# A recurrent kernel's step: two gates in one PSUM bank, wider products, and another order on VectorE

## The chip, the cores and the metric

The kernel runs on one core of a Trainium2 chip. TensorE (PE) multiplies, with its weight loads in a queue of their own (PEld); VectorE (DVE) and ScalarE (ACT) do the elementwise work; GpSimd (POOL) and SyncE (SP) start transfers. PE writes its sums to PSUM, which has eight banks of 512 float32 values in each of 128 partitions. The metric is the device time in microseconds of one execution, as the median of several runs. Everything is in float32.

## The reference

`x` is 16 sequences of 256 steps with 512 features. A GRU runs over the steps from a given state, and a router with 16 experts (one shared weight matrix) works on all of its states. Cut to what matters:

```python
def cell(h, x):
    gi = x @ W_ih + b_ih
    gh = h @ W_hh + b_hh
    i_r, i_z, i_n = jnp.split(gi, 3, axis=-1)
    h_r, h_z, h_n = jnp.split(gh, 3, axis=-1)
    r = sigmoid(i_r + h_r)
    z = sigmoid(i_z + h_z)
    n = tanh(i_n + r * h_n)
    return (1.0 - z) * n + z * h

# then, on the states as 4096 rows of 512:
S = softmax(states @ router_w + router_b)       # 16 experts
G, idx = top_k(S.T, 256)                        # each expert takes 256 rows
y[idx] += G * (states[idx] @ expert_w + expert_b)
return x + y
```

The 256 steps depend on each other: the products `h @ W_hh` of a step need the state that the step before it made.

## The kernel before, in words

**The state's form.** The 512 features are four chunks of 128, and `hs` holds the state with the features on the partitions: `hs[:, k, slot, :]` is chunk k for the 16 sequences. It is the stationary operand, with 16 columns, and `W_hh` is streamed past it. A product with 16 or 32 columns fills only a strip of PE's array, so `h_part` issues four products with `tile_position=(0, 32*j)`, one per strip of 32 columns. Strip j makes every fourth block of 32 output features (`columns`), and its result lies in partitions 32j onward. The 512 features of one gate thus lie as 128 partitions by 128 columns.

Two steps share a set of sums: an even step uses 16 rows of each strip; the odd step after it gives PE both states (32 columns) and uses the other 16. `p, odd = divmod(s, 2)`; the sums of pair p are in column half `p % 2` of a bank. Before the change each gate has a bank: `r_bank`, `n_bank`, `z_bank`, of which columns 0 to 255 are used. `rr`, `hn`, `zz` are the two halves of each.

**What is added to the sums.** The part of x for a pair is made six pairs ahead by `x_part`, in products of 384 columns (three gates) into `x_bank0` or `x_bank1`, and `x_done` on DVE adds biases and puts it into a ring in SBUF. ACT copies it into the sums before the recurrent products add to them: `preset_first` for r, `preset_rest` for n's bias and for z. For n, x's part stays in the ring, since r multiplies only the recurrent part.

**One step.** The order on PE, ACT, DVE, POOL and SP in the step loop is the order of the calls (a manual schedule); the framework adds a semaphore wait wherever one engine needs another's result, or a place that another engine still uses. PE runs the first half of the contraction (chunks 0, 1, `first`) for r and for n, then the second half (`second`) for r and for n, and then all of z:

```python
for ks in (first, second):
    h_part(s, "r", ks)
    h_part(s, "n", ks)
h_part(s, "z", range(KC))
```

So the first products need only the first half of the state's features. After them PE does work that does not hang on this step: half of an `x_part` (L403) and, in most steps, one unit of an expert's product for an earlier group of states (`expert`, L370); some steps have router products instead (`logits`, L305).

ACT: sigmoid of r (L505), in even steps `preset_first` (L386), two tanh, one for each half of the features (L557), sigmoid of z (L558), in even steps `preset_rest` (L389, L396), in some steps a `gather` (L293).

DVE: `seen` (L509), a copy of a single value of r, so that DVE has waited for ACT before its next instruction waits for PE; r times n's sums by halves (L553); plus x's part (L555); and then ten small instructions, five for each half: `turn_n` transposes n in 32 by 32 blocks (L565), `turn_z` transposes z (L568), `less_n` makes h - n (L571), `by_z` multiplies by z (L576), `plus_n` adds n and writes the half of the next state (L579). After that come `x_done` in odd steps, an expert's results, and transposes of x.

POOL and SP: SP starts the loads of x, some of which POOL lets go by a small copy that reads the newest state (L219, L617).

**After the steps** the last router products, softmax, a search for each expert's 256th value, and the output follow; several expert products are left for then (`late_part`, L108).

Of the kernel before, what the change touches and what calls it, by code (L numbers as in the profile page):

```python
# [8 lines left out]
F32 = mybir.dt.float32  # L9
# [3 lines left out]
AF = mybir.ActivationFunctionType  # L13
# [4 lines left out]
def kernel(  # L18
# [15 lines left out]
    nc = tc.nc  # L34
    B, T, D = x.shape
    E = router_w.shape[1]
    P = 128
    QD = 32
    KC = D // P
# [118 lines left out]
    with (  # L158
# [9 lines left out]
        def slot(s):  # L168
# [3 lines left out]
        whh = wts.tile([P, KC, 3, D], F32, name="whh")  # L172
# [9 lines left out]
        ones = wts.tile([2, QD], F32, name="ones")  # L182
        nc.vector.memset(ones, 1.0)

        r_bank, n_bank, z_bank, x_bank0, x_bank1, l_bank = banks = [
            ps_g.tile([P, D], F32, name=f"gates{i}") for i in range(6)
        ]
        rr, hn, zz = ([bank[:, P * i : P * (i + 1)] for i in range(2)] for bank in (r_bank, n_bank, z_bank))
        lgt = l_bank[:, 0:P]

        def quadrant(j, m=QD):
            return slice(QD * j, QD * j + m)

        def columns(ap, j):

            return ap.rearrange("p (c j i) -> p j c i", j=KC, i=QD)[:, j]

        def load_rows(dst, src, form):

            rows = src.rearrange(form, c=KC)  # L200
            for h in range(2):
                ks = slice(KC // 2 * h, KC // 2 * (h + 1))
                queues[h].dma_start(out=dst[:, ks, :], in_=rows[:, ks, :])
# [33 lines left out]
        with tc.manual_schedule(engines={ET.SP, ET.Activation, ET.Pool}):  # L237
            def load_gate(dst, src, form, i, gate):
                load_rows(dst[:, :, i, :], src[:, gate * D : (gate + 1) * D], form)

            def load_k(k):
                rows = w_ih.rearrange("(p c) n -> p c n", c=KC)
                to = wih.rearrange("p c g d -> p c (g d)")
                for h, queue in enumerate(queues):
                    cols = slice(3 * HD * h, 3 * HD * (h + 1))
                    queue.dma_start(out=to[:, k, cols], in_=rows[:, k, cols])

            nc.sync.dma_start(out=xs[:, 0, :], in_=x[:, 0:TG, :])
            load_k(0)
            nc.scalar.dma_start(out=c0, in_=cond)  # L250
            load_k(1)
            load_k(2)
            nc.scalar.dma_start(out=xs[:, 1, :], in_=x[:, TG : 2 * TG, :])
            load_k(3)
            for gate in (0, 2, 1):
                load_gate(whh, w_hh, "(c p) n -> p c n", gate, gate)
            nc.scalar.activation(dummy, ones[0:1, 0:1], AF.Sigmoid)
            for dst, src in (
                (b_raw[0:1], b_ih.rearrange("(o g d) -> o g d", o=1, d=D)),
                (b_raw[1:2], b_hh.rearrange("(o g d) -> o g d", o=1, d=D)),  # L260
                (b_n, b_hh[2 * D :].rearrange("(o d) -> o d", o=1)),
            ):
                nc.gpsimd.dma_start(out=dst, in_=src)
            for j in range(KC):
                load_xa(2, xa2, j, (nc.sync, nc.sync))
            nc.sync.dma_start(out=ewr[:, :, E:], in_=expert_w.rearrange("(c p) n -> p c n", c=KC))
            nc.sync.dma_start(out=ewr[:, :, 0:E], in_=router_w.rearrange("(c p) n -> p c n", c=KC))
            nc.gpsimd.dma_start(out=rb, in_=router_b.rearrange("(o e) -> o e", o=1).to_broadcast([P, E]))
            nc.sync.dma_start(out=eb, in_=expert_b.rearrange("(o d) -> o d", o=1).to_broadcast([P, D]))
# [145 lines left out]
                ring[:, p % AHEAD, :, :], bank[:, 0 : 3 * P].rearrange("p (g d) -> p g d", d=P), bias[:, 0:3, :], ALU.add  # L415
            )

        def h_part(s, gate, ks):
            p, odd = divmod(s, 2)
            m = QD if odd else B  # L420
            dst, gate_ = {"r": (rr[p % 2], 0), "z": (zz[p % 2], 1), "n": (hn[p % 2], 2)}[gate]
            for k in ks:

                lhs = hs[:, k, slot(s) - odd : slot(s) + 1, :].rearrange("p t b -> p (t b)")
                for j in range(KC):
                    nc.tensor.matmul(  # L426
                        dst[quadrant(j, m)],
                        lhs,
                        columns(whh[:, k, gate_, :], j),
                        start=False,  # L430
                        stop=(k == KC - 1),
                        tile_position=(0, QD * j),
                        skip_group_check=True,
                    )
# [8 lines left out]
        with tc.manual_schedule(engines={ET.PE, ET.Activation, ET.DVE}):  # L443
            for bank in banks:
                begin_sums(bank)
            keep_clock(8)
            held = (r_bank, n_bank, z_bank, x_bank0, x_bank1)

            def spread_x(g, bank):
                xT[g] = xtp.tile([P, TG // 2, P], F32, name="xt")  # L450
                for c in range(KC):
                    nc.tensor.transpose(bank[:, P * c : P * (c + 1)], xs[:, g, c::KC], ident)
                for q in range(TG // 2):
                    to = xT[g][:, q, :].rearrange("p (c o b) -> p c o b", c=KC, b=B)
                    nc.vector.tensor_copy(
                        to, bank.rearrange("p (c b t) -> p c t b", c=KC, t=TG)[:, :, 2 * q : 2 * q + 2, :]
                    )

            spread_x(0, idles[0])
            keep_clock(2, (idles[1],))  # L460
            for k in range(KC):
                for p in range(KC):
                    x_part(p, k, held[p], start=False)
                if k == 1:
                    for c in range(KC):
                        nc.tensor.transpose(
                            idles[1][:, B * c : B * (c + 1)], c0[:, P * c : P * (c + 1)], ident[0:B, 0:B]
                        )
                    nc.vector.tensor_copy(
                        hs[:, :, 0, :], idles[1][:, 0 : KC * B].rearrange("p (k b) -> p k b", b=B)  # L470
                    )
                elif k == 2:
                    biases(l_bank)
                    nc.vector.tensor_copy(bias, l_bank.rearrange("p (g d) -> p g d", d=P))
            spread_x(1, idles[0])
            for p in range(KC):
                x_done(p, held[p])
                if p == 0:
                    preset_first(0)
                elif p == 2:  # L480
                    preset_rest(0)
            for k in range(KC):
                x_part(KC, k, held[KC], start=False)
            x_done(KC, held[KC])
            keep_clock(2)
# [3 lines left out]
        first, second = range(KC // 2), range(KC // 2, KC)  # L489

        with tc.manual_schedule(engines={ET.PE, ET.Activation, ET.DVE, ET.Pool, ET.SP}):
# [4 lines left out]
            for s in range(T):  # L496
                p, odd = divmod(s, 2)
                g, c = divmod(s, TG)
                for ks in (first, second):
                    h_part(s, "r", ks)  # L500
                    h_part(s, "n", ks)
                h_part(s, "z", range(KC))

                r = gp.tile([P, P], F32, name=f"r{odd}")
                nc.scalar.activation(r, rr[p % 2], AF.Sigmoid)  # L505
# [30 lines left out]
                if s >= T - 2:  # L536
                    expert_for(4)

                halves = [
                    (half, slice(QD * ks[0], QD * (ks[-1] + 1)), slice(ks[0], ks[-1] + 1))  # L540
                    for half, ks in enumerate((first, second))
                ]
                t, nT, zT = (
                    [gp.tile([P, P // 2], F32, name=f"{name}{half}") for half in range(2)]
                    for name in (f"t{odd}", "nT", "zT")
                )
# [1 line left out]
                    [gp.tile([P, KC // 2, B], F32, name=f"{name}{half}") for half in range(2)]  # L548
                    for name in ("u", "v")
                )  # L550
                zs = gp.tile([P, P], F32, name=f"zs{odd}")
                for half, cols, ks in halves:
                    nc.vector.tensor_tensor(t[half], r[:, cols], hn[p % 2][:, cols], ALU.mult)  # L553
                for half, cols, ks in halves:
                    nc.vector.tensor_tensor(t[half], t[half], ring[:, p % AHEAD, 2, cols], ALU.add)  # L555
                for half, cols, ks in halves:
                    nc.scalar.activation(t[half], t[half], AF.Tanh)  # L557
                nc.scalar.activation(zs, zz[p % 2], AF.Sigmoid)  # L558
                if not odd and p < T // 2 - 1:
                    preset_rest(p + 1)  # L560
                if g and c < KC:
# [3 lines left out]
                    nc.vector.transpose(nT[half], t[half])  # L565

                def turn_z(half):
                    nc.vector.transpose(zT[half], zs[:, halves[half][1]])  # L568

                def less_n(half):  # L570
                    nc.vector.tensor_tensor(  # L571
# [9 lines left out]
                    )  # L581

                for f, half in (
                    (turn_n, 0), (turn_n, 1), (less_n, 0), (turn_z, 0), (less_n, 1),
                    (by_z, 0), (plus_n, 0), (turn_z, 1), (by_z, 1), (plus_n, 1),
                ):
                    f(half)

# [24 lines left out]
                if cx >= KC and gx + 2 < NG:  # L613
                    if cx == KC:
                        xa_next = new_xa()
                    j = cx - KC
# [27 lines left out]
    with (  # L644
# [80 lines left out]
        with tc.manual_schedule(engines={ET.PE, ET.Activation, ET.DVE}):  # L725

            bank = ps_s.tile([P, D], F32, name="bank", tag="s")
# [42 lines left out]
            gate = gate_of(pg)  # L770
# [3 lines left out]
            for i, (g, cols) in enumerate(items):  # L774
# [4 lines left out]
                if step == 1:  # L779
                    n = ps_n.tile([P, 1], F32, name="n", tag="n")  # L780
# [14 lines left out]
        with tc.If(again > 0):  # L795
# [51 lines left out]
            gate = gate_of(pg)  # L847
# [39 lines left out]
```

## Time and profile before

| | |
|---|---|
| time, median of 3 runs | 1165.82 us (1165.52 to 1165.89) |
| the profiled execution: its own time, and the span of its trace | 1166.15 us, 1164.4 us |
| granted clock of TensorE | full in all slices of the span |
| from the first to the last sigmoid of r (255 steps apart) | 27.8 to 1089.9 us of the span |
| recurrent products, L426 | 24,576 of 128 columns, 724.7 us busy |
| x's part, L403 | 4,064 of 384 columns, 379.6 us busy |
| sigmoid of r, L505, and of z, L558 | 256 of each, 278 ns each |
| tanh, L557 | 512, 249 ns each |
| transposes of n, L565, and of z, L568 | 512 of each, 234 and 240 ns each |
| last sum, L579 | 512, 192 ns each |

The profile is of one execution. "Busy" counts time in which at least one instruction of the group was under way; neighbours overlap, so it is less than the number times the mean. Products on PE are pipelined, and a product that waits for its turn in the array is not told from one that runs. Therefore the distance between starts says more than busy time, and I use the recorded start of single instructions where a turn of the step loop is measured.

### The profile page before, as it was taken

What the parts mean: (1) busy time and instruction counts of PE and PEld (TensorE: products, weight loads), DVE (VectorE), ACT (ScalarE), POOL (GpSimd) and SP (SyncE); (2) the same over time, 40 slices, a digit from 0 to 9 for tenths busy, and PEclk for the clock granted to TensorE, in tenths of its full rate; (3) what the DMA queues carried; (4) which work ended last, traced back from release to release, by engine and by line L of the source; (5) the groups of instructions that cost most, each with busy time, mean ns of one, the idle gap of its engine ahead of it and who ended that gap; (6) DMA issues with size and microseconds to landing.
All of it is one profiled execution on the core that took longest, in us unless ns stands there. A gap on an engine that the chain in (4) does not pass through costs nothing.

```text
span 1164.4 us, 72051 instructions
## 1 busy us (share of the span) xinstructions
PE 1148.1 (99%) x32271; PEld 925.2 (79%) x32271; DVE 769.0 (66%) x4229; ACT 387.0 (33%) x1590; POOL 42.5 (4%) x240
## 2 busy tenths in 40 slices
PE   8999999999999999999999999999999999998898
PEld 4778888888888888888888888888888888888762
DVE  2666667666666666666676666666666666665674
ACT  1233333333333333333333333333333333333420
POOL 1000000000000000000000000000000000000000
PEclk9999999999999999999999999999999999999999
DMA  8100000000000000000000000000000000000126
GB/s 268 38 13 17 21 20 19 16 21 22 20 20 21 19 20 17 21 22 20 20 19 20 19 18 20 22 21 20 20 20 19 20 8 13 4 5 4 48 69 227
DMA packets 43818, 37.02 MB, mean 32 GB/s; under 512 B 6992, under 2 KB 35424, under 8 KB 43504
## 3 DMA queue, kind: packets, MB, share of 16 engines
q1 hardware_dynamic: 41808, 28.89, 8.4%
q8 instruction: 255, 4.18, 1.5%
q10 hardware_dynamic: 1568, 3.44, 0.9%
q14 instruction: 59, 0.48, 0.1%
q0 software_dynamic: 128, 0.02, 0.1%
HBM read 23.94 MB, written 8.39 MB: 28 GB/s over the span
## 4 chain that ended last, share of the span: by engine, by line
PE 95%; DVE 3%; DMA 1%; ACT 1%; issue 0%; SPq 0%; ACTq 0%; DVEq 0%
PE gates L426 57%; PE gates L403 27%; PE pe L108 5%; PE pe L370 5%; DMA wih<-in_L_cond_W_ih_dram 1%; PE gates L305 1%; DVE zT L568 0%; DVE nT L565 0%; DVE t L553 0%; ACT r L505 0%; ACT t L557 0%; DVE hs L579 0%; DVE v L576 0%; PE idle L403 0%; DVE u L571 0%
## 5 line engine op out<-in xcount | busy, mean ns | idle before, releaser
L426 PE MATMUL gates<-whh,hs 128*16 128x128 f32 x24576 | 724.7, 273 | 5.0 <-DVE zT L568 2.5
L426 PEld LDWEIGHTS gates<-whh,hs 128*16 128x16 f32 x24576 | 672.0, 103 | 37.6 <-ACT ht L293 15.8
L403 PE MATMUL gates<-wih,xt 128*32 128x384 f32 x4064 | 379.6, 486 | 1.9 <-DMA wih<-in_L_cond_W_ih_dram 1.6
L505 ACT ACTIVATE r<-gates 128x128 f32<-128x128 f32 x256 | 71.1, 278 | 551.9 <-PE gates L426 551.7
L403 PEld LDWEIGHTS gates<-wih,xt 128*32 128x32 f32 x4064 | 144.4, 110 | 91.4 <-issue 84.3
L509 DVE COPY seen<-r 1x1 f32<-1x1 f32 x256 | 36.3, 142 | 268.0 <-ACT r L505 267.9
L557 ACT ACTIVATE t<-t 128x64 f32<-128x64 f32 x512 | 103.2, 249 | 136.1 <-DVE t L555 136.1
L565 DVE STREAM_TRANSPOSE nT<-t 128x64 f32<-128x64 f32 x512 | 100.4, 234 | 47.8 <-ACT t L557 47.8
L568 DVE STREAM_TRANSPOSE zT<-zs 128x64 f32<-128x64 f32 x512 | 122.7, 240 | 0.6 <-ACT zs L558 0.6
L370 PEld LDWEIGHTS pe<-ewr,ht 128*32 128x32 f32 x1920 | 69.1, 110 | 62.3 <-issue 60.1
L579 DVE TENSOR_TENSOR hs<-v,nT 128x32 f32<-128x32 f32 x512 | 98.3, 192 | 17.4
L576 DVE TENSOR_TENSOR v<-u,zT 128x32 f32<-128x32 f32 x512 | 98.7, 193 | 8.8
L370 PE MATMUL pe<-ewr,ht 128*32 128x128 f32 x1920 | 92.0, 273 | 0.7 <-issue 0.7
L555 DVE TENSOR_TENSOR t<-t,xs 128x64 f32<-128x64 f32 x512 | 90.7, 219 | 0.0
L553 DVE TENSOR_TENSOR t<-r,gates 128x64 f32<-128x64 f32 x512 | 90.3, 218 | 0.0
L571 DVE TENSOR_TENSOR u<-hs,nT 128x32 f32<-128x32 f32 x512 | 78.2, 153 | 0.0
L558 ACT ACTIVATE zs<-gates 128x128 f32<-128x128 f32 x256 | 71.2, 278 | 1.8 <-ACT t L557 0.6
L414 DVE TENSOR_TENSOR xs<-gates,bias 128x384 f32<-128x384 f32 x127 | 69.7, 551 | 0.5 <-PE gates L403 0.5
L108 PE MATMUL pe<-ewr,ht 128*32 128x128 f32 (+2 forms) x1320 | 64.3, 343 | 0.0
L108 PEld LDWEIGHTS pe<-ewr,ht 128*32 128x32 f32 x1320 | 36.9, 110 | 20.5 <-issue 18.5
L293 ACT COPY ht<-hs 128x128 f32<-128x128 f32 (+1 forms) x128 | 52.2, 410 | 0.8 <-DVE hs L579 0.8
L228 DVE STREAM_TRANSPOSE xt<-xa 128x256 f32<-128x256 f32 x58 | 38.7, 668 | 6.5 <-issue 6.5
(106 smaller groups left out, 300.0 us busy)
## 6 DMA issues: line engine op xcount, KB each, us to landing
out_dram<-xs SPq DMA_DIRECT2D x31, 256.0 KB, 3.7
xa<-in_x_dram SPq DMA_DIRECT2D x232, 32.0 KB, 1.9
xs<-in_x_dram SPq DMA_DIRECT2D x100, 64.0 KB, 2.2
xs<-in_x_dram SPq DMA_DIRECT2D x6, 256.0 KB, 3.9
wih<-in_L_cond_W_ih_dram ACTq DMA_DIRECT2D x4, 384.0 KB, 7.9
wih<-in_L_cond_W_ih_dram SPq DMA_DIRECT2D x4, 384.0 KB, 10.7
whh<-in_L_cond_W_hh_dram SPq DMA_DIRECT2D x3, 512.0 KB, 12.8
whh<-in_L_cond_W_hh_dram ACTq DMA_DIRECT2D x3, 512.0 KB, 9.6
```

The source lines that it names most:

```text
L108: nc.tensor.matmul(pe[q, cols], ht[:, g, k, q], ewr[:, k, E:][:, cols], start=False, stop=(k == KC - 1), tile_position=(0, QD * j), skip_g ...
L370: nc.tensor.matmul(pes[g][quadrant(j), at : at + P], ht[:, g, k, quadrant(j)], ewr[:, k, E + P * quarter : E + P * (quarter + 1)], start=F ...
L403: nc.tensor.matmul(bank[quadrant(j), at], lhs, columns(wih[:, k, gates, :].rearrange("p g d -> p (g d)"), j), start=start and k == 0, stop ...
L426: nc.tensor.matmul(dst[quadrant(j, m)], lhs, columns(whh[:, k, gate_, :], j), start=False, stop=(k == KC - 1), tile_position=(0, QD * j), ...
L553: nc.vector.tensor_tensor(t[half], r[:, cols], hn[p % 2][:, cols], ALU.mult)
L555: nc.vector.tensor_tensor(t[half], t[half], ring[:, p % AHEAD, 2, cols], ALU.add)
L557: nc.scalar.activation(t[half], t[half], AF.Tanh)
L565: nc.vector.transpose(nT[half], t[half])
L568: nc.vector.transpose(zT[half], zs[:, halves[half][1]])
L571: nc.vector.tensor_tensor(u[half], hs[:, halves[half][2], slot(s), :], of_step(nT[half], odd), ALU.subtract)
L576: nc.vector.tensor_tensor(v[half], u[half], of_step(zT[half], odd), ALU.mult)
L579: nc.vector.tensor_tensor(hs[:, halves[half][2], slot(s + 1), :], v[half], of_step(nT[half], odd), ALU.add)
```

## The change

Three things are changed in the step, and one follows from them.

1. r and n of a pair share a bank. There are still two banks for them, but they are now told apart by the pair and not by the gate: `rn_bank0` holds r (columns 0 to 127) and n (128 to 255) of even pairs, `rn_bank1` those of odd pairs. `W_hh` is stored in the order r, n, z, so that r's and n's columns for a contraction chunk stand side by side. In the first contraction half `h_part(s, "rn", first)` then makes both in products of 256 columns. The second half is made apart as before, r ahead of n.
2. The last contraction chunk of z is made in two halves of 64 columns, first for the first half of the features. z's sigmoid is made in two instructions of 64 columns, and each stands behind the tanh of its half on ACT.
3. The ten small instructions on DVE have another order: the transpose of z's first half goes ahead of that of n's second half, and the other work on the second half later.

```diff
-        r_bank, n_bank, z_bank, x_bank0, x_bank1, l_bank = banks = [
+        rn_bank0, rn_bank1, z_bank, x_bank0, x_bank1, l_bank = banks = [
             ps_g.tile([P, D], F32, name=f"gates{i}") for i in range(6)
         ]
-        rr, hn, zz = ([bank[:, P * i : P * (i + 1)] for i in range(2)] for bank in (r_bank, n_bank, z_bank))
+        rn = [bank[:, 0 : 2 * P] for bank in (rn_bank0, rn_bank1)]
+        rr, hn = ([both[:, P * i : P * (i + 1)] for both in rn] for i in range(2))
+        zz = [z_bank[:, P * i : P * (i + 1)] for i in range(2)]
...
-            for gate in (0, 2, 1):
-                load_gate(whh, w_hh, "(c p) n -> p c n", gate, gate)
+            for i, gate in enumerate((0, 2, 1)):
+                load_gate(whh, w_hh, "(c p) n -> p c n", i, gate)
...
-        def h_part(s, gate, ks):
+        def h_part(s, gate, ks, half=None):
             p, odd = divmod(s, 2)
             m = QD if odd else B
-            dst, gate_ = {"r": (rr[p % 2], 0), "z": (zz[p % 2], 1), "n": (hn[p % 2], 2)}[gate]
+            dst, gates = {
+                "rn": (rn[p % 2], slice(0, 2)),
+                "r": (rr[p % 2], slice(0, 1)),
+                "n": (hn[p % 2], slice(1, 2)),
+                "z": (zz[p % 2], slice(2, 3)),
+            }[gate]
+            cs = slice(None) if half is None else slice(KC // 2 * half, KC // 2 * (half + 1))
+            at = slice(None) if half is None else slice(QD * cs.start, QD * cs.stop)
             for k in ks:
...
                     nc.tensor.matmul(
-                        dst[quadrant(j, m)],
+                        dst[quadrant(j, m), at],
                         lhs,
-                        columns(whh[:, k, gate_, :], j),
+                        columns(whh[:, k, gates, :].rearrange("p g d -> p (g d)"), j)[:, cs],
...
-            held = (r_bank, n_bank, z_bank, x_bank0, x_bank1)
+            held = (rn_bank0, rn_bank1, z_bank, x_bank0, x_bank1)
...
-                for ks in (first, second):
-                    h_part(s, "r", ks)
-                    h_part(s, "n", ks)
-                h_part(s, "z", range(KC))
+                h_part(s, "rn", first)
+                h_part(s, "r", second)
+                h_part(s, "n", second)
+                h_part(s, "z", range(KC - 1))
+                for half in range(2):
+                    h_part(s, "z", (KC - 1,), half)
...
-                zs = gp.tile([P, P], F32, name=f"zs{odd}")
+                zs = [gp.tile([P, P // 2], F32, name=f"zs{odd}{half}") for half in range(2)]
...
                 for half, cols, ks in halves:
                     nc.scalar.activation(t[half], t[half], AF.Tanh)
-                nc.scalar.activation(zs, zz[p % 2], AF.Sigmoid)
+                    nc.scalar.activation(zs[half], zz[p % 2][:, cols], AF.Sigmoid)
...
                 def turn_z(half):
-                    nc.vector.transpose(zT[half], zs[:, halves[half][1]])
+                    nc.vector.transpose(zT[half], zs[half])
...
                 for f, half in (
-                    (turn_n, 0), (turn_n, 1), (less_n, 0), (turn_z, 0), (less_n, 1),
-                    (by_z, 0), (plus_n, 0), (turn_z, 1), (by_z, 1), (plus_n, 1),
+                    (turn_n, 0), (turn_z, 0), (less_n, 0), (turn_n, 1), (by_z, 0),
+                    (turn_z, 1), (plus_n, 0), (less_n, 1), (by_z, 1), (plus_n, 1),
                 ):
                     f(half)
```

## Prediction

> **What bounds the kernel now.** I read the page's busy times and its list of costliest groups first, then the chain that ended last, then the timeline of one pair of steps. From the page:
>
> ```profile
> PE 1148.1 (99%) x32271; PEld 925.2 (79%) x32271; DVE 769.0 (66%) x4229; ACT 387.0 (33%) x1590; POOL 42.5 (4%) x240
> ...
> L426 PE MATMUL gates<-whh,hs 128*16 128x128 f32 x24576 | 724.7, 273 | 5.0 <-DVE zT L568 2.5
> ...
> L505 ACT ACTIVATE r<-gates 128x128 f32<-128x128 f32 x256 | 71.1, 278 | 551.9 <-PE gates L426 551.7
> ```
>
> L426 has 24,576 instructions in 256 steps: 96 a step, two for each call of `h_part`'s loop. The chain gives their pace (start in us, length in us):
>
> ```profile
> 603.92 2.62 PE gates L426 x96
> 606.55 1.29 PE gates L403 x16
> 607.84 2.79 PE gates L426 x96
> ```
>
> Four products, one per 32-column strip of the array, run together; I call them a round. 96 products are 24 rounds: 2.62/24 = 109.2 ns. L403's 16 are 4 rounds of 384 columns: 1.29/4 = 322.5 ns. The line through both is 0.833 ns a column plus 2.5 ns a round.
>
> PE at 99% is not the whole truth. The timeline (start, length):
>
> ```profile
> 603.72 2.83 PE L426 MATMUL gates<-whh,hs 128*32 128x128 f32 x96
> 603.90 0.19 DVE L579 TENSOR_TENSOR hs<-v,nT 128x32 f32<-128x32 f32 x1
> 605.29 0.28 ACT L505 ACTIVATE r<-gates 128x128 f32<-128x128 f32 x1 [1.84 <-PE gates L426]
> 605.60 0.14 DVE L509 COPY seen<-r 1x1 f32<-1x1 f32 x1 [1.51 <-ACT r L505]
> 605.73 0.35 DVE L553 TENSOR_TENSOR t<-r,gates 128x64 f32<-128x64 f32 x2
> 606.00 0.35 DVE L555 TENSOR_TENSOR t<-t,xs 128x64 f32<-128x64 f32 x2
> ...
> 606.25 0.40 ACT L557 ACTIVATE t<-t 128x64 f32<-128x64 f32 x2 [0.68 <-DVE t L555]
> ...
> 606.54 0.39 DVE L565 STREAM_TRANSPOSE nT<-t 128x64 f32<-128x64 f32 x2 [0.18 <-ACT t L557]
> ...
> 606.66 0.28 ACT L558 ACTIVATE zs<-gates 128x128 f32<-128x128 f32 x1
> ...
> 607.48 0.19 DVE L579 TENSOR_TENSOR hs<-v,nT 128x32 f32<-128x32 f32 x1
> ...
> 607.81 1.94 PE L426 MATMUL gates<-whh,hs 128*16 128x128 f32 x64
> ```
>
> A step's loop is: products, r's sigmoid, `seen`, r times n, plus x's part, tanh, transposes, first half of the new state, next step's products. Here the state ends at 607.67 and the products follow at 607.81, 0.146 us later. So this turn is set by the chain through ACT and DVE, not by PE. Over all 256 steps (starts of L505, ends of L579): 52 of the 255 turns have this 0.146 us between state and products and average 4.08 us; in the others the state is early and PE's work sets the turn, 166 of them at 4.13 us, with an expert's unit on PE, and 26 at 4.35 to 4.56. The spare time in the 4.13 turns is small: 26 ns after odd steps, some 85 after even ones. **A delay of the chain of more than that shows in every step.**
>
> The chain, from the step's first product: r's sigmoid starts at +1.560 us (even steps) or +1.574 (odd, after a stall); from there to the end of the first half of the state 2.328 (even) or 2.378 (odd); then 0.146. Sums 4.034 and 4.098, as the 52 turns have.
>
> **The change, part by part.**
>
> *r and n in one bank.* Before, r's sigmoid waits for r's last product alone and reads r's bank while PE goes on with n in another: n's second half is four rounds, 4 x 109.2 = 437 ns, and they lie beside the sigmoid and `seen` (605.29 + 0.437 = 605.73, just where L553 starts). After, r's sigmoid reads a bank into which those products write. In the built program its wait counts to the last product of n's second half, where it counted to the last of r's. So the 437 ns that were hidden come ahead of the sigmoid. Here a rule is to be weighed. The row above would cost the move at nothing: r's data are ready at the same place in PE's order. The Trainium skill (PSUM — Partial Sum Buffer, "PSUM bank collisions raise a hardware error") says that an engine must not touch a bank's 32-partition quadrant while TensorE writes it, other columns or not, and to guard PSUM by bank. By the row the sum for this part is 0, by the rule +437 ns a step. No run here shows a collision, but the wait is in the program, and I take the rule. Behind the sigmoid on ACT stand the preset of r (even steps), both tanh and z's sigmoids; DVE's `seen` and all that follows wait for it, and PE for the state.
>
> *256-column products.* In the first half 8 rounds of 109.2 become 4 of 0.833 x 256 + 2.5 = 215.8: 10.4 ns less a step, ahead of the sigmoid. R's start moves by 437 - 10 = +0.426: 1.986 and 2.000.
>
> *z's last quarter by halves.* 2 rounds of 109.2 become 4 of 64 columns. By the line 55.8 each: +4.8 ns of PE. A rule speaks against that: the Trainium skill (TensorE: Matmul & The Clock Gate, "Wait — 56ns, not 53.3ns?") says that starts of products never come closer than about 25 ns. 16 x 25 = 400 ns instead of 223 would be +182. But in this trace three products to other strips go out in a row that is hardly longer than one of them (297 ns):
>
> ```profile
> 1091.10 0.31 PE L108 MATMUL pe<-ewr,ht 128*32 128x128 f32 x3
> ```
>
> Two gaps in some 13 ns, 7 ns each, so I take 4.8. Upper end: weight loads (110 ns each in L403's rows) held to a round each keep 109.2, +213; lower end: nothing. PE's turn is 4.12 us then, 4.34 at the upper end; both are under the chain below, so it costs nothing in the usual turns.
>
> *z's sigmoid by halves.* z's bank is likewise waited for whole (the first half's wait counts to the second half's last product), but with r late z is done before tanh. ACT gets one more instruction between the tanhs. Successive 64-column ACT instructions start 162 ns apart here, so first half of z's sigmoid at tanh + 0.162, second tanh at + 0.324. tanh and sigmoid already alternate with no table load in the loop. In odd steps a separate semaphore instruction stands ahead of z's sigmoid; when it was the last to be released it cost 60 ns. Now its semaphore is long up: between 0 and 60, I take 0, since ACT is busy with tanh for longer.
>
> *VectorE's order.* Up to the first transpose nothing changes: sigmoid to L553 0.437, to tanh 0.522, to L565 0.288, sum 1.247. From there, by start-to-start times of the trace: transpose to transpose 169, transpose to subtraction 147, subtraction to transpose 73, transpose to product 161, product to transpose 109, transpose to sum 164, and the sum lasts 192: 1015 ns. No operand is later than that: the first z half ends at tanh + 0.162 + 0.240 and may be turned 31 ns later, at 1.392 after the sigmoid's start; its place is 1.416. Before it took 1081 (even) and 1132 (odd), the latter because z's sigmoid came late. Gain 66 and 117 ns. The state's second half follows 0.52 us later (109 + 186 + 227), before it was 0.61; PE needs it 0.86 us after the first products.
>
> *The rest.* The recurrent weights' six loads keep queues and order; only their place in `whh` changes. Presets, `gather`, `x_done`, and what POOL and SP issue keep their order behind the step; each hangs on the state and moves with it. Presets for the next pair go to the other bank, which nobody touches.
>
> *Sum.* Even 1.986 + 1.247 + 1.015 + 0.146 = 4.394 us, odd 2.000 + 2.408 = 4.408. PE's 4.12 lies beneath it with 0.28 us to spare, so the 52 short turns and the 4.13 turns all take this length. 12 turns are longer already (4.43 to 6.11) and keep theirs. 243 x 4.401 = 1069.5, plus the 12, 56.6: 1126.1 us, where the 255 turns took 1062.1. That is +64.0; the step outside the count adds 0.4. The span becomes 1164.4 + 64.4 = 1228.8; the profiled execution took 1166.15, 1.75 more than its span, and the median of the runs is 0.33 below it: 1230.2. I predict **1230**.
>
> **Rivals.**
>
> *The bank costs nothing* (the other sign): the sigmoid is in effect released with r's own products. Then even and odd chains are 4.034 - 0.010 - 0.066 = 3.958 and 3.971; every turn falls back to PE's work: 5.6 ns off 191 turns and some 0.12 us off the 52, -7 us: **1159**. For it speaks that r is ready early; against it the wait in the program. It decides as long as the delay at the sigmoid stays under about 0.16 us (4.13 - 3.97); the wait asks for 0.43.
>
> *The delay is partly made good*: n's tail or DVE's part is shorter than their rows say, by 0.1 us a step: **1206**. Against it: in nearly all steps each of these times stays within 5 ns of its median.
>
> *ACT or PE are dearer as well*: 60 ns in odd steps are 127 x 0.06 = +7.5; the z rounds at 109.2 lengthen the turns with logits, +5.6: together **1243**. Nothing in the rows asks for it.
>
> *PE becomes the bound through the short products and the bank costs nothing*: 0.2 us in every turn, +35: **1201**. The 7 ns row speaks against it.
>
> **How the numbers follow.** The likeliest, a chain lengthened by the bank, 0.87: 1222 to 1238 of its own. Dearer 0.05, partly made good 0.03, PE's short products 0.02, bank at no cost 0.03. Range 1214 to 1244 leaves out about one in ten. Faster 0.03; within 0.2% (2.3 us, about what a measurement of this kernel tells from no change) 0.01; slower 0.96.
>
> **What would show it.** r's sigmoid about 1.99 us after the step's first product, and after it `seen` and L553's counterpart at once, no longer just at n's end; turns of 4.39 and 4.41 us at nearly all steps, with or without a unit; PE idle some 0.25 us ahead of each step's first product, ended by DVE's state; first transpose to first state 1.015 us; 215.8 ns for a round of 256 and 55.8 for one of 64 columns. Wrong if r's sigmoid still starts at 1.55, if L553's gap behind it grows, or if turns stay at 4.12.

## The result

The changed kernel takes 1181.96 us (median of 4 runs, 1180.97 to 1182.68), the kernel before 1165.70 in the same comparison: a ratio of 1.0139, 95% interval 1.0121 to 1.0156. It is slower by 1.4%, as forecast in kind, but by a quarter of the forecast amount: +16.3 us where the working gave +64.

The page of the changed kernel (the lines of the program are some ten higher now: L426 is L435, L505 is L516, L553 L564, L557 L568, L558 L569, L565 L576, L579 L590):

```profile
PE 1159.7 (98%) x30223; PEld 821.0 (70%) x30223; DVE 697.9 (59%) x4229; ACT 366.8 (31%) x1846; POOL 42.7 (4%) x240
...
L435 PE MATMUL gates<-whh,hs 128*16 128x128 f32 (+1 forms) x22528 | 720.5, 283 | 9.8 <-DVE u L582 2.8
...
L516 ACT ACTIVATE r<-gates 128x128 f32<-128x128 f32 x256 | 71.1, 278 | 598.0 <-PE gates L435 598.0
```

Each step has 88 recurrent products instead of 96. ACT waits for them 598.0 us in all instead of 551.7: 46 us more ahead of r's sigmoid. The timeline from the end of an even step through the odd one after it (start, length in us):

```profile
604.07 0.15 DVE L590 TENSOR_TENSOR hs<-v,nT 128x32 f32<-128x32 f32 x1
...
604.36 2.82 PE L435 MATMUL gates<-whh,hs 128*32 128x256 f32 x88
...
606.37 0.28 ACT L516 ACTIVATE r<-gates 128x128 f32<-128x128 f32 x1 [1.55 <-PE gates L435]
606.67 0.14 DVE L520 COPY seen<-r 1x1 f32<-1x1 f32 x1 [1.32 <-ACT r L516]
606.75 0.33 DVE L564 TENSOR_TENSOR t<-r,gates 128x64 f32<-128x64 f32 x2
...
607.25 0.26 ACT L568 ACTIVATE t<-t 128x64 f32<-128x64 f32 x1 [0.60 <-DVE t L566]
...
607.41 0.21 ACT L569 ACTIVATE zs<-gates 128x64 f32<-128x64 f32 x1
607.51 0.25 ACT L568 ACTIVATE t<-t 128x64 f32<-128x64 f32 x1
607.53 0.24 DVE L576 STREAM_TRANSPOSE nT<-t 128x64 f32<-128x64 f32 x1 [0.18 <-ACT t L568]
...
607.70 0.20 DVE L579 STREAM_TRANSPOSE zT<-zs 128x64 f32<-128x64 f32 x1
...
607.83 0.18 DVE L582 TENSOR_TENSOR u<-hs,nT 128x32 f32<-128x32 f32 x1
607.92 0.24 DVE L576 STREAM_TRANSPOSE nT<-t 128x64 f32<-128x64 f32 x1
...
608.08 0.15 DVE L587 TENSOR_TENSOR v<-u,zT 128x32 f32<-128x32 f32 x1
608.15 0.24 DVE L579 STREAM_TRANSPOSE zT<-zs 128x64 f32<-128x64 f32 x1
...
608.31 0.15 DVE L590 TENSOR_TENSOR hs<-v,nT 128x32 f32<-128x32 f32 x1
...
608.52 1.71 PE L435 MATMUL gates<-whh,hs 128*16 128x256 f32 x40
```

r's sigmoid starts 2.01 us after the step's first product (604.36 to 606.37), where it was 1.57 (603.72 to 605.29). `seen` follows 0.30 us later, as before. The chain through ACT and DVE now sets nearly every turn (the time from one step's start to the next one's), with an expert's unit on PE or without: from the starts of r's sigmoids, 110 turns are of 4.24 to 4.25 us and 115 of 4.15, in alternation, against 166 of 4.13 before. Another 17 are of 4.34: there PE has router products or two units and still sets the turn. The working had 4.394 and 4.408. What came out shorter can be read from the same rows. L564 follows `seen` by 0.08 us, not 0.13. From the first transpose to the end of the state's first half it is 607.53 to 608.46, 0.93 and not 1.015. After the odd step the next product follows the state by 0.06 us (608.46 to 608.52), after the even one by 0.14 (604.22 to 604.36).

Medians over steps 12 to 239, from the starts of single instructions, in us:

| | before, even / odd | predicted, even / odd | after, even / odd |
|---|---|---|---|
| first product to r's sigmoid | 1.571 / 1.574 | 1.986 / 2.000 | 1.998 / 2.002 |
| r's sigmoid to first transpose of n | 1.247 / 1.247 | 1.247 / 1.247 | 1.169 / 1.169 |
| first transpose to end of the state's first half | 1.081 / 1.132 | 1.015 / 1.015 | 0.929 / 0.929 |
| state to next step's first product, where the chain sets the turn | 0.146 / 0.146 | 0.146 / 0.146 | 0.146 / 0.054 |
| turn | 4.128 / 4.128 | 4.394 / 4.408 | 4.242 / 4.154 |

### The profile page after: what moved, and what is told of

Its sections match the earlier page's. It is cut to its first block, busy times and chain, and to the rows that moved or that the text cites. A ratio compares the mean times of both kernels' runs of the same rounds, so it can differ in the third digit from the quotient of the medians.

```text
span 1180.8 us, 68084 instructions
## 1 busy us (share of the span) xinstructions
PE 1159.7 (98%) x30223; PEld 821.0 (70%) x30223; DVE 697.9 (59%) x4229; ACT 366.8 (31%) x1846; POOL 42.7 (4%) x240
## 4 chain that ended last, share of the span: by engine, by line
PE 92%; DVE 4%; ACT 2%; DMA 1%; issue 0%; SPq 0%; ACTq 0%; DVEq 0%
PE gates L435 57%; PE gates L405 25%; PE pe L108 5%; PE pe L372 4%; DVE nT L576 1%; DMA wih<-in_L_cond_W_ih_dram 1%; ACT r L516 1%; ACT t L568 1%; DVE t L564 1%; DVE zT L579 1%; PE gates L307 1%; DVE u L582 0%; DVE t L566 0%; DMA xs<-in_x_dram 0%; DVE seen L520 0%
## 5 line engine op out<-in xcount | busy, mean ns | idle before, releaser
L435 PE MATMUL gates<-whh,hs 128*16 128x128 f32 (+1 forms) x22528 | 720.5, 283 | 9.8 <-DVE u L582 2.8
L435 PEld LDWEIGHTS gates<-whh,hs 128*16 128x16 f32 x22528 | 601.2, 103 | 147.8 <-DVE hs L590 19.0
L516 ACT ACTIVATE r<-gates 128x128 f32<-128x128 f32 x256 | 71.1, 278 | 598.0 <-PE gates L435 598.0
L405 PEld LDWEIGHTS gates<-wih,xt 128*32 128x32 f32 x4064 | 122.4, 110 | 97.7 <-issue 94.0
L568 ACT ACTIVATE t<-t 128x64 f32<-128x64 f32 x512 | 128.9, 252 | 132.9 <-DVE t L566 132.9
L576 DVE STREAM_TRANSPOSE nT<-t 128x64 f32<-128x64 f32 x512 | 123.7, 242 | 48.1 <-ACT t L568 48.1
L579 DVE STREAM_TRANSPOSE zT<-zs 128x64 f32<-128x64 f32 x512 | 111.9, 219 | 0.1
L569 ACT ACTIVATE zs<-gates 128x64 f32<-128x64 f32 x512 | 107.8, 211 | 0.1
L587 DVE TENSOR_TENSOR v<-u,zT 128x32 f32<-128x32 f32 x512 | 87.6, 171 | 8.9
L590 DVE TENSOR_TENSOR hs<-v,nT 128x32 f32<-128x32 f32 x512 | 87.7, 171 | 8.7
L582 DVE TENSOR_TENSOR u<-hs,nT 128x32 f32<-128x32 f32 x512 | 91.7, 179 | 0.0
L564 DVE TENSOR_TENSOR t<-r,gates 128x64 f32<-128x64 f32 x512 | 84.2, 200 | 0.0
```

The lines of the kernel that those rows point to most:

```text
L405: nc.tensor.matmul(bank[quadrant(j), at], lhs, columns(wih[:, k, gates, :].rearrange("p g d -> p (g d)"), j), start=start and k == 0, stop ...
L435: nc.tensor.matmul(dst[quadrant(j, m), at], lhs, columns(whh[:, k, gates, :].rearrange("p g d -> p (g d)"), j)[:, cs], start=False, stop=( ...
L569: nc.scalar.activation(zs[half], zz[p % 2][:, cols], AF.Sigmoid)
L579: nc.vector.transpose(zT[half], zs[half])
L582: nc.vector.tensor_tensor(u[half], hs[:, halves[half][2], slot(s), :], of_step(nT[half], odd), ALU.subtract)
L587: nc.vector.tensor_tensor(v[half], u[half], of_step(zT[half], odd), ALU.mult)
```

## The experiments

Theory A, formed on this trace: the wait on the shared bank costs what its rounds say, and is partly paid back by three terms that the working took too large. The rivals are stated with each run. In the diffs `...` stands for lines left out. The time of the kernel before was 1166.02 us beside the first four and 1166.77 beside the other four.

**1. The bank alone.** z and VectorE's order as before.

```diff
-                h_part(s, "z", range(KC - 1))
-                for half in range(2):
-                    h_part(s, "z", (KC - 1,), half)
+                h_part(s, "z", range(KC))
...
-                    nc.scalar.activation(zs[half], zz[p % 2][:, cols], AF.Sigmoid)
+                nc.scalar.activation(zs, zz[p % 2], AF.Sigmoid)
...
-                    (turn_n, 0), (turn_z, 0), (less_n, 0), (turn_n, 1), (by_z, 0),
-                    (turn_z, 1), (plus_n, 0), (less_n, 1), (by_z, 1), (plus_n, 1),
+                    (turn_n, 0), (turn_n, 1), (less_n, 0), (turn_z, 0), (less_n, 1),
+                    (by_z, 0), (plus_n, 0), (turn_z, 1), (by_z, 1), (plus_n, 1),
```

> r and n share a bank and the first contraction half has 256-column products, as in the change; z's last quarter and sigmoid are whole and VectorE has the order of before. Theory A (the bank's wait moves r's sigmoid 0.43 us back, and z's sigmoid by halves together with VectorE's new order give part of it back): the first transpose starts 1.17 us after r's sigmoid as in the changed kernel, the end of the first half of the state comes 2.25 us after it instead of 2.10, turns of 4.39 and 4.31 us instead of 4.24 and 4.15, about 1219 us. Theory B (the wait simply costs less than its four rounds, and the other edits gave nothing back): 1182 us.

1216.80 us, ratio 1.0433 (1.0412 to 1.0453). Its timeline:

```profile
602.05 0.28 ACT L514 ACTIVATE r<-gates 128x128 f32<-128x128 f32 x1 [2.55 <-PE gates L435]
...
602.43 0.33 DVE L562 TENSOR_TENSOR t<-r,gates 128x64 f32<-128x64 f32 x2
...
603.22 0.39 DVE L574 STREAM_TRANSPOSE nT<-t 128x64 f32<-128x64 f32 x2 [0.19 <-ACT t L566]
603.24 0.26 ACT L567 ACTIVATE zs<-gates 128x128 f32<-128x128 f32 x1
...
603.88 0.19 DVE L585 TENSOR_TENSOR v<-u,zT 128x32 f32<-128x32 f32 x1
...
604.10 0.19 DVE L588 TENSOR_TENSOR hs<-v,nT 128x32 f32<-128x32 f32 x1
```

L562 starts 0.38 us after r's sigmoid here too, so that gain comes with the bank and not with the new order. The state ends 2.249 us after the sigmoid instead of 2.097, and the turns are 4.392 and 4.304. Product and sum are next to each other in this order and last 0.19 us each; in the changed kernel, with a transpose between them, 0.15. The other two edits together gave back 0.15 us a step, 35 us in all (1216.80 less 1181.96).

**2. Everything but the bank.** r and n in their own banks, 128-column products; z by halves and the new order stay.

```diff
+        rr, hn, zz = ([bank[:, P * i : P * (i + 1)] for i in range(2)] for bank in (r_bank, n_bank, z_bank))
...
-                h_part(s, "rn", first)
-                h_part(s, "r", second)
-                h_part(s, "n", second)
+                for ks in (first, second):
+                    h_part(s, "r", ks)
+                    h_part(s, "n", ks)
```

> z's last quarter and sigmoid by halves and VectorE's new order, as in the change, but r and n in banks of their own and all products of r and n of 128 columns. Theory A: r's sigmoid is again 1.57 us after the first product, L553's counterpart 0.437 us after that, held by n; z's sums end 1.31 us after r's sigmoid and hold z's sigmoid, so the new order has nothing to gain: the state 2.32 to 2.40 us after r's sigmoid (2.33 and 2.38 before), 1166 us, give or take 2. Theory B (the new order alone shortens the chain by 66 to 117 ns, as the prediction's rival with a free bank has it): 1159 to 1161 us.

1168.71 us, ratio 1.0020 (1.0013 to 1.0027): slightly slower than before, and 0.7 us above the range that was expected. An even step:

```profile
601.12 0.28 ACT L513 ACTIVATE r<-gates 128x128 f32<-128x128 f32 x1 [1.97 <-PE gates L432]
...
601.56 0.35 DVE L561 TENSOR_TENSOR t<-r,gates 128x64 f32<-128x64 f32 x2
...
602.44 0.22 ACT L566 ACTIVATE zs<-gates 128x64 f32<-128x64 f32 x1
...
602.69 0.25 DVE L576 STREAM_TRANSPOSE zT<-zs 128x64 f32<-128x64 f32 x1
...
603.32 0.15 DVE L587 TENSOR_TENSOR hs<-v,nT 128x32 f32<-128x32 f32 x1
```

L561 is back at 0.44 us after the sigmoid, held by n: the semaphore count that stands for n's last product is reached 24 ns before it starts. z's sigmoid starts 1.32 us after r's, when z's sums are complete, so the second instruction of the new order waits until 602.69, where by the pace of the changed kernel (0.169 us after n's first transpose, which starts at 602.37) it could have started at 602.54. The state ends at 2.347 (even) and 2.407 (odd), no sooner than before. The short z products show in the turns: 4.133 us where PE sets them, 5 ns more than before. The prediction's rival with a free bank had 1159; with r released, this kernel is at 1168.7, and the 10 ns a turn that wide products would save are 2.5 us of it. Since everything but the bank and its products is in this kernel, the rest of the change's cost, 13 us, is the bank's with its wide products, net of what it gives back. With the old order behind it the same bank costs 51 us (experiment 1, 1216.80 against 1166.02): its price hangs on what stands behind it.

**3. All products of r and n in 256 columns.** If r's sigmoid waits for n's last product, r need not come first.

```diff
-                h_part(s, "rn", first)
-                h_part(s, "r", second)
-                h_part(s, "n", second)
+                h_part(s, "rn", range(KC))
```

> The changed kernel with the second contraction half of r and n in 256-column products too. Theory A (r's sigmoid waits for n's last product anyway): r's sigmoid comes 10 ns earlier in the step, 1179.5 us. Theory B (r's sigmoid is released by r's own products and something else is late): r's data come 0.43 us later than in the changed kernel, every turn longer by as much, up to 1280 us.

1180.56 us, ratio 1.0123 (1.0101 to 1.0145). r's sigmoid starts at 1.987 and 1.991 us, 11 ns sooner, and turns are 4.231 and 4.143. r's own last product ends some 0.43 us later in this kernel than in the changed one, and nothing is lost by it: the sigmoid does wait for n. The traces say the same: in the changed kernel the sigmoid starts 67 ns after the end of n's last product and 503 ns after that of r's, in the kernel before 57 ns after r's and ahead of n's (medians; ends of products are modelled).

**4. One wait less on the odd step's first product.** A copy of one value on ScalarE, from the bank that x's part writes next, so that PE, by its products of x's part, has waited for ScalarE before the step's end.

```diff
+            touched = gp.tile([1, 1], F32, name="touched")
...
                 if x_for:
+                    if not odd:
+                        nc.scalar.copy(touched, x_bank[0:1, 0:1])
                     for k in second if odd else first:
```

> The changed kernel with one more small ScalarE copy (one value of the bank of x's part, in even steps, after r's sigmoid); x's part on PE then waits for ScalarE long before it matters, and the first product of the odd step has one wait instead of two, so no separate semaphore instruction. Theory A (that instruction is the 92 ns by which the product follows the state later after even steps, 146 against 54 ns): even turns 4.15 instead of 4.24 us, 1171 us. Theory B (the 92 ns come from the 32 stationary columns of odd steps): 1182 us or a little more.

1173.24 us, ratio 1.0062 (1.0042 to 1.0082), 2 us more than expected, in part because the odd steps' sigmoid came 9 ns later (122 x 9 ns is 1.1 us); why it did stays open. What changes is in the view of the recurrent products' line, in the row of PE's separate semaphore instructions (count, min/median/max ns). The kernel before:

```profile
L426 PEldq EVENT_SEMAPHORE  x258: 51/51/51, 23.6 to 1087.8; - x129
```

the changed kernel:

```profile
L435 PEldq EVENT_SEMAPHORE  x131: 51/51/239, 23.3 to 1104.1; - x131
```

this one:

```profile
L435 PEldq EVENT_SEMAPHORE  x9: 51/51/241, 22.0 to 1094.0; - x9
```

Before, every step had one ahead of its first product, which waited both for DVE's state and for ACT. In the changed kernel only odd steps have it, as even steps begin in the other bank. Here nearly none has it, and the first product follows the state by 54 ns after both kinds of step; the even turns fall from 4.242 to 4.151. It was not the 32 stationary columns. The semaphore events of the changed kernel show where the time goes: the separate instruction takes the late wait, the one for DVE. It starts 39 ns after the state's end and lasts 51, and the product follows 56 ns after it.

**5 and 6. One of the other two edits undone.** First z whole, with the new order kept (the parts of experiment 1's diff that concern z); then the old order with z by halves (its last part).

> The changed kernel with z's last quarter and z's sigmoid whole again, the sigmoid behind both tanh; VectorE's new order stays. Theory A (the new order needs z early, so it is worth something only with z by halves): z's sigmoid starts 1.19 us after r's and ends at 1.47, so the second instruction of the new order, z's transpose, waits until 1.50 instead of 1.34; the state 2.26 instead of 2.10 us after r's sigmoid, turns of 4.40 and 4.31, 1220 us. Theory B (the two edits each give back a part of their own): about 1199 us.

> The changed kernel with VectorE's order of before; z's last quarter and sigmoid stay in halves. Theory A: the second tanh now stands behind the first half of z's sigmoid, and the old order needs it second: n's second transpose waits until 1.43 us after r's sigmoid instead of 1.34, and by_z and plus_n stand next to each other again; the state 2.34 us after r's sigmoid, turns of 4.49 and 4.40, 1241 us. Theory B (each edit gives back a part of its own): about 1199 us.

1216.96 us, ratio 1.0434 (1.0418 to 1.0450), and 1241.82 us, ratio 1.0648 (1.0632 to 1.0665). With z whole the new order is worth nothing: its state ends at 2.254 us after r's sigmoid, that of experiment 1 at 2.249. With z by halves the old order is 25 us worse than with z whole. The timeline of this second run:

```profile
602.41 0.28 ACT L516 ACTIVATE r<-gates 128x128 f32<-128x128 f32 x1 [2.30 <-PE gates L435]
...
603.46 0.21 ACT L569 ACTIVATE zs<-gates 128x64 f32<-128x64 f32 x1
603.56 0.25 ACT L568 ACTIVATE t<-t 128x64 f32<-128x64 f32 x1
603.58 0.50 DVE L576 STREAM_TRANSPOSE nT<-t 128x64 f32<-128x64 f32 x2 [0.19 <-ACT t L568]
...
604.57 0.19 DVE L590 TENSOR_TENSOR hs<-v,nT 128x32 f32<-128x32 f32 x1
```

The second tanh stands behind half of z's sigmoid, so the two transposes of n, which the old order wants first, take 0.50 us instead of 0.39. Behind the shared bank the two edits are one: each needs the other.

**7. A version built of these pieces.** The changed kernel with experiments 3 and 4 in it, z's last products whole on PE (its sigmoid stays by halves), and without `seen`: r's sigmoid has waited for n, so r times n needs only one wait.

```diff
-                h_part(s, "rn", first)
-                h_part(s, "r", second)
-                h_part(s, "n", second)
-                h_part(s, "z", range(KC - 1))
-                for half in range(2):
-                    h_part(s, "z", (KC - 1,), half)
+                h_part(s, "rn", range(KC))
+                h_part(s, "z", range(KC))
...
-                nc.vector.tensor_copy(seen[0:1, s % 8 : s % 8 + 1], r[0:1, 0:1])
...
+                    if not odd:
+                        nc.scalar.copy(touched, x_bank[0:1, 0:1])
```

> The changed kernel with all products of r and n in 256 columns, z's last quarter whole on PE (its sigmoid stays in halves), the small ScalarE copy that takes the second wait off the odd step's first product, and without the copy of one value of r on VectorE, which is not needed when r's sigmoid has waited for n. Theory A (the chain is the sum of these pieces): chain 1.99 + 2.03 + 0.05 = 4.07 us, below PE's 4.107 us for a step with an expert's unit, which sets most turns; 1161 to 1163 us, faster than both kernels. Theory B (r times n cannot start sooner than 0.38 us after r's sigmoid): turns of 4.15 us, about 1171 us.

1161.41 us, ratio 0.9956 (0.9943 to 0.9970): 0.4% faster than the kernel before, and faster than the changed one. From its timeline:

```profile
603.76 0.28 ACT L512 ACTIVATE r<-gates 128x128 f32<-128x128 f32 x1 [1.95 <-PE gates L435]
604.07 0.35 DVE L560 TENSOR_TENSOR t<-r,gates 128x64 f32<-128x64 f32 x2 [1.82 <-ACT r L512]
```

r times n starts 0.31 us after r's sigmoid, and the state ends at 2.046. The state ends 86 ns before the next product, 32 more than where the chain sets the turn (54); so PE sets the turn again, at 4.108 us in most steps with a unit: 4.128 less two times 10.4 ns.

**8. The kernel before with the small copy.** In every step, as all of them have the double wait.

> The kernel before with the small ScalarE copy in every step ahead of x's part, so that the first product of a step has one wait. Theory A (the separate semaphore instruction is worth 92 ns wherever the chain sets the turn): the 52 short turns come down from 4.08 to some 3.99 us, the 4.13 us turns stay, 1161 us. Theory B (the 146 ns between state and product belong to the product's start itself): 1166 us.

1161.48 us, ratio 0.9960 (0.9947 to 0.9974). The turns that PE sets stay at 4.13 us; the short ones come down to 3.99 us on average, with clusters at 3.96 and 4.00. In 43 of the 50 turns under 4.11 us the product now follows the state by 54 or 55 ns, where it was 146 or 147. So about 5 us lay in that semaphore instruction without any other edit, and experiment 7's version, with the shared bank and all its wide products, is no faster than this one: the two cannot be told apart.

## Why the prediction was right in kind and wrong in size

That r's sigmoid comes to wait for n, and by how much, was right. The step that failed is the sum of the chain behind it, where three terms were carried over from the old kernel too large: 1.247 us from the sigmoid to the first transpose (measured 1.169), 1.015 us for VectorE's order (0.929), and 0.146 us from the state to the next product (0.054 after odd steps).

*r and n in one bank*: right. The sigmoid came 0.438 (even) and 0.428 us (odd) later in the step than in the short turns before, for a forecast of 0.426, and experiments 2 and 3, with the semaphore events, show that it is n's products in the same bank. Most of the 12 ns beyond the forecast in even steps lies in their first round, which took 226 ns and not 216. The wait in the built program is the reason, and it is what the Trainium skill (PSUM — Partial Sum Buffer, "PSUM bank collisions raise a hardware error") asks for; no run shows what would come without it.

*256-column and 64-column products*: right. In an odd step of the changed kernel rounds start 215, 109 and 55 to 56 ns apart. PE's short products did not come near the upper ends of the working. (One of these is a slip: four rounds of 109.2 in the place of two are +218 ns, not +213. Nothing hung on it.)

*"Up to the first transpose nothing changes", 1.247 us*: wrong by 78 ns. L553 started 127 ns after `seen` before. The prediction itself notes that n was complete "just where L553 starts", and among its signs has the counterpart come "at once", yet it took the 0.437 us for the pace of the instructions. It was n that held L553: the semaphore count for n's last product was reached 22 to 24 ns before L553 started, in each of the steps 12 to 239, and in the changed kernel it is reached 0.40 us before L564 starts. So L564 follows `seen` by 71 ns, 56 less. The pair of sums runs 22 ns closer too; in experiment 7, where r times n again has a wait of its own, it is back at the old pace. Thus 56 ns of the bank's wait had been in the chain already: counted twice.

*VectorE's order, 1015 ns*: wrong by 86. The times from start to start came from the old order. Its rows, in an odd step of the kernel before:

```profile
607.14 0.15 DVE L571 TENSOR_TENSOR u<-hs,nT 128x32 f32<-128x32 f32 x1
607.25 0.19 DVE L576 TENSOR_TENSOR v<-u,zT 128x32 f32<-128x32 f32 x1
607.48 0.19 DVE L579 TENSOR_TENSOR hs<-v,nT 128x32 f32<-128x32 f32 x1
607.59 0.24 DVE L568 STREAM_TRANSPOSE zT<-zs 128x64 f32<-128x64 f32 x1
```

Here product and sum of the first half each stand behind another elementwise instruction and last 192 to 193 ns, and the transpose starts 109 to 110 ns after the sum does. In the new order each stands behind a transpose of the other half and lasts 150 to 151, and the next instruction starts 70 ns after it does. The transpose 39 ns closer, the shorter sum with 41, and its start 6 ns closer (158 after that transpose, not 164) make the 86. The row for the subtraction, 153 ns, which also stood behind a transpose, was the nearer one. What sets these lengths stays open. It is not only whether an instruction reads what the one before it made: L576 above lasts 193 ns behind a subtraction that it does not read, and in the new order the first subtraction lasts 177 behind z's transpose, but 150 in experiment 2, where that transpose had to wait.

*"Then 0.146"*: wrong by 92 ns for the turns after odd steps. The prediction took the time from state to product for a constant of the engines. It held a separate semaphore instruction, which the change takes away where a step begins in the other bank (experiments 4 and 8).

*The semaphore instruction ahead of z's sigmoid in odd steps, 0 to 60*: 0 was right; z's sigmoid starts 162 to 163 ns after tanh in both kinds of step.

The sum with these: even turns 4.394 - 0.078 - 0.086 + 0.012 for the sigmoid's 1.998 = 4.242, odd 4.408 - 0.078 - 0.086 - 0.092 + 0.002 = 4.154. That is 0.203 us less on the average of the two, over 243 turns 49 us: 1230 becomes 1181. The range was too narrow because all three errors have one sign: each was a time measured under the old kernel's waits and neighbours and carried over as a fixed cost, where a lower end without it belonged. The nearest rival, "the delay is partly made good", had the kind right, but with 0.1 us a step half of the size, and a chance of 0.03; what speaks against it there, that these times hardly vary, does not show that they are fixed costs.

## What to carry to other kernels

Before moving a wait to the head of a chain, look at what the chain already waits for behind it: if another input arrives at the very moment an instruction starts, that instruction's delay is a wait, and it is not to be charged a second time. Take an elementwise instruction's time from a row with the same neighbours: the same operation lasted 151 ns in one order and 192 in another. Count the waits on the instruction that closes a loop; a second one cost 92 ns here, and an earlier instruction of the same engine can take it over.

## What the runs showed of the hardware

A product with two waits got a separate semaphore instruction ahead of it, recorded at 51 ns, and followed its late input by 146 ns; with one wait it followed by 54. On VectorE the first half's 128x32 product and sum lasted 192 to 193 ns behind another elementwise instruction, with the next instruction 109 to 110 ns after the sum's start, and 150 to 151 ns behind a transpose, with the next one after 70. Rounds of four 64-column float32 products, one per strip of 32 columns, started 55 to 56 ns apart, on the same line as those of 128, 256 and 384 columns.
